# Adjacency blocks stored with the identity on their diagonal, and 16-bit operands for the put-off counts, in a four-layer graph network

## The chip, the cores and the metric

The kernel runs on one core of a Trainium2 chip. The metric is the device time of one execution in microseconds (us). The times shown are of nine executions, and one further execution was profiled.

A core has five engines that run side by side, each with its own queue of instructions that it takes in order. TensorE (PE in the profile) multiplies matrices; a matmul has a weight load (PEld) ahead of it, which can overlap the matmul before. VectorE (DVE), ScalarE (ACT) and GpSimd (POOL) work on tiles of 128 partitions. SyncE (SP) issues transfers; ScalarE and GpSimd issue some too. The transfers themselves run on 16 DMA engines. Results of matmuls land in PSUM, which has eight banks per partition; everything else on the chip lies in SBUF.

## The reference

The input is `x` (4096 rows of 256 features) and a symmetric 0/1 matrix `adj` (4096 x 4096) whose diagonal is all ones. Four layers follow one another, each with a residual sum and a LayerNorm:

```python
x = _layernorm(x + _L0_gnn_ref(x, adj, L0_gnn_W, L0_gnn_b))
x = _layernorm(x + _L1_gnn_ref(x, adj, W1, W2, W3, U1, U2, ln_g, ln_b))
x = _layernorm(x + _L2_gnn_ref(x, adj, adj, L2_gnn_weight, L2_gnn_bias))
x = _layernorm(x + _L3_gnn_ref(x, adj, L3_gnn_W, L3_gnn_b))
```

- Layer 0: `agg = adj @ x / deg`, then `relu([x, agg] @ W + b)`.
- Layer 1, two steps: `Xf = R @ Xf` with `R` the rows of `adj + I` divided by their sums, and `Xa = A @ Xa`, where `A` is the softmax of bilinear attention logits cut to the smallest set of entries that holds 0.9 of each row, and renormalised. `Z` sums `Xf @ U1[n].T + Xa @ U2[n].T`; the layer ends with its own LayerNorm of `X + Z`.
- Layer 2: `[x, adj @ x, e] @ weight + bias`, where `e_i = sum_j adj_ij adj_ji`.
- Layer 3: `A_hat = adj + I`, normalised on both sides by the square root of its row sums, times `x`, then `relu(. @ W + b)`.

So layers 1 and 3 need `adj + I`, layers 0 and 2 need `adj` alone.

## The kernel before

There are 32 row tiles of 128 rows (`NT`), and `adj` is taken in blocks of 128 x 128. A product with `adj` is always made in the same way. The right-hand side is split in two halves of fewer bits each, laid side by side as 512 columns of the type `fp32r`. The 0/1 blocks, transposed, are the weights. So one row tile is 32 matmuls of 128x512, one for each block of its row of `adj`, which add up in one PSUM bank; the two halves of 256 columns are then added.

**The order of the work.** The program text is written tile by tile, but the order of each engine's queue is set when the program is built, from dependencies, the order in the text and reckoned durations. A queue's order can therefore differ from the text's, and the profile shows the order that came out. Waits between engines, and for buffers to be free again, are added by the builder.

**Layer 0** (`l0_main`, L271, and the loop at L338). For each tile `it`, GpSimd issues two transfers (L276) that read the tile's blocks from HBM as 32-bit numbers and write them to SBUF as 8-bit ones, `a8`; one transfer brings blocks 0 to 15, the other blocks 16 to 31. Nine buffers serve the `a8` tiles and, at the start, the tiles of `x`. SyncE stores each half to `adj8_d` in HBM (L277), from where the later layers read it. ScalarE casts 8 blocks at a time to `fp32r` (L281), PE multiplies (L173), and DVE counts the ones of each column (`column_counts`, L287) on the 8-bit tile. `l0_degrees` (L304) turns the counts into degrees by a small 16-bit matmul (L306). `l0_agg` (L317, DVE) reads the PSUM bank of the finished product; two banks (`acc`, `nef`) take turns. `l0_end` (L323) makes the LayerNorm: `ln_stats` (L188) computes mean and variance on DVE and takes the variance to the power -0.5 on GpSimd (`rstd`, L197); `ln_apply` (L200) on DVE waits for it. SyncE then stores `x1` and `x1b` (L331, L332). `l0_keys` makes attention keys of a tile two turns later.

**Layer 1** (`run_step`, L941, twice). `pieces` (L720) interleaves, in eight groups, the attention logits of the tile after next, the attention product of the current tile, and the product with `adj + I` of one tile (`neighbours`, L674). `neighbours` reads `adj8_d` (L678), casts it on ScalarE (L680) and multiplies (L683); after the last group it adds one more matmul, with the identity `ident_r` as weights (L685), which turns `adj` into `adj + I`. In step 0 it also makes `adj @ adj` for the diagonal block (L693), of which `r_end` (L700) takes the diagonal (L707) as `nef`, the `e_i` of layer 2. In step 0 the attention product uses the 16 largest entries of each row, whose rows GpSimd gathers from HBM (`gather`, L666, eight slots `G`); in step 1 it is a dense product (L766). 

`pick` (L531) marks rows for which this did not suffice in `bad`, a 0/1 column. `flag` (L579) counts them: two matmuls with one column each, with the weights `ones_sq` (how many in the tile, L589) and `before` (how many ahead of each row, L590), all 32-bit. The profile shows each of them as two records. The rows are put on a list (L603) and done later, 128 at a time (`put_off`, L894). PE takes part in `flag` in the midst of its other work, so it waits for `bad` when that is late.

At the end of step 1, beside the put-off rows of the list, `zu_tile` (L874) makes for every tile the products of its layer 2 input with two parts of the weight: SyncE loads the tile, PE transposes and multiplies (`zu`, L862, into 512 columns), ScalarE copies the result from PSUM to one of four slots `out` (L871), and SyncE stores it to `zu_d` (L878). For put-off rows the store is a GpSimd scatter (L787). Columns 0 to 255 are what `adj` multiplies in layer 2; columns 256 to 511 are the tile's own part `u`.

**Layers 2 and 3** (from L1101). `load_halves` reads the first half of `zu_d` and splits it. `main` (L1121) multiplies with the blocks of `adj8_d` (`piece`, L1102). `l2_end` (L1126) adds `u` and the `nef` term and makes the LayerNorm. `l2_y` makes the right-hand side of layer 3, `y`. `l3_end` (L1154) scales the product, and adds the tile's own `y` in two steps (the two halves, L1160 to L1162), since layer 3 needs `adj + I`; the loop at L1161 has three DVE steps of which the third adds the second half of the product.

## Time and profile before

| what | us |
|---|---|
| median of nine executions (3236.24 to 3254.3) | 3243.18 |
| the profiled execution's own time | 3243.96 |
| its span, first to last instruction | 3242.3 |
| PE busy | 2956.1 |
| DVE busy | 2289.4 |
| ACT busy | 1745.5 |
| POOL busy | 786.7 |
| mean granted TensorE clock | 0.966 of full speed |

By stages, from the trace: layer 0 is over after some 350 us, step 0 of layer 1 runs to about 1300, the change from step 0 to step 1 to about 1440, step 1 with its put-off rows to 2700, layer 2 to 2997 and layer 3 to the end.

How to read it: busy times are of one execution, and a busy PE is not PE at its peak, since matmuls are pipelined and the records of neighbours overlap. In a timeline row the first number is the start in us from the span's start and the second the duration of the row, which may be several instructions ("x4"); what stands in brackets is how long the engine was idle before it and what ended that. The name in "L276" is the kernel's line. Transfers that an engine issues are shown at their issue, not at their landing. A share over the whole span mixes stages with different limits, so each part of a change is read in its own stage.

### The profile page before, as it was taken

Reading aid. Unit: us, or ns where it says so; the run is one execution under the profiler, and the core shown is the slowest. Engines: PE = TensorE matmul, PEld = TensorE weight load, DVE = VectorE, ACT = ScalarE, POOL = GpSimd, SP = SyncE. Lnnn points to the kernel's source line nnn. Section 1 sums busy time; section 2 is a strip of 40 time slices with the busy share of each in tenths; the row PEclk is TensorE's granted clock in tenths of the full one; section 3 lists DMA queues with packets and bytes.
Section 4 is the critical chain, followed back from the end, with each engine's and each line's share of the span. In section 5 each row is a group of like instructions: output and inputs, shape, how many; then the busy total and the mean of one; then the engine's idle time right before and its main releaser. Section 6 shows DMA issues by size and latency. Waiting matters only on the chain. (4 is left out here: it accounts for less than half of the span.)

```text
span 3242.3 us, 45754 instructions
## 1 busy us (share of the span) xinstructions
PE 2956.1 (91%) x14376; PEld 2333.2 (72%) x14376; DVE 2289.4 (71%) x7161; ACT 1745.5 (54%) x2906; POOL 786.7 (24%) x915
## 2 busy tenths in 40 slices
PE   7999889999999996799989899999999796999998
PEld 3788667777777774577877777877788554887886
DVE  4566778888888785268979896989799663444444
ACT  3555655566656563375545454645555334666664
POOL 1121256676666664000000001000100100000000
PEclk9999999999999997899999999999999898999999
DMA  9995467778777774320001110011011234333332
GB/s 169 157 176 118 85 108 141 141 147 141 140 139 140 138 137 130 110 67 22 24 25 27 30 38 27 29 35 38 25 35 29 64 125 132 108 109 102 104 110 81
DMA packets 247872, 300.14 MB, mean 93 GB/s; under 512 B 34688, under 2 KB 201536, under 8 KB 247616
## 3 DMA queue, kind: packets, MB, share of 16 engines
q0 software_dynamic: 46576, 104.94, 23.1%
q1 hardware_dynamic: 188800, 180.93, 18.7%
q10 hardware_dynamic: 12240, 11.23, 1.1%
q8 instruction: 116, 1.90, 0.3%
q14 instruction: 140, 1.15, 0.2%
HBM read 331.17 MB, written 66.45 MB: 123 GB/s over the span
## 5 line engine op out<-in xcount | busy, mean ns | idle before, releaser
L683 PE MATMUL acc_r<-xh,adjq 128*128 128x512 f32 x2048 | 609.6, 428 | 30.0 <-ACT adjq L680 16.0
L766 PE MATMUL acc_bank<-xa,at 128*128 128x256 f32 x2304 | 568.6, 387 | 28.8 <-ACT at L744 28.3
L669 POOL DMA_INDIRECT G<-x_d,cols x512 | 496.8, 970 | 279.4 <-PE acc_bank L758 148.2
L680 ACT CAST adjq<-adj 128x512 fp32r<-128x512 fp8e4 x512 | 316.4, 620 | 392.3 <-PE acc_r L683 304.8
L766 PEld LDWEIGHTS acc_bank<-xa,at 128*128 128x128 f32 x2304 | 424.0, 194 | 90.1 <-ACT at L744 39.1
L683 PEld LDWEIGHTS acc_r<-xh,adjq 128*128 128x128 f32 x2048 | 376.3, 191 | 126.2 <-ACT adjq L680 46.0
L197 POOL TENSOR_TENSOR rstd<-ve,mhalf 128x1 f32<-128x1 f32 x168 | 103.1, 614 | 1345.1 <-DVE ve L195 1237.4
L430 DVE MAX8 cand<-e 128x8 f32<-128x256 f32 x1024 | 382.5, 413 | 65.0 <-ACT e L412 63.7
L412 ACT COPY e<-lg 128x512 f32<-128x512 f32 x552 | 319.6, 585 | 198.4 <-PE lg L411 194.7
L411 PE MATMUL lg<-kS,q 128*128 128x512 f32 x1104 | 399.8, 447 | 4.8 <-ACT e L412 4.8
L758 PE MATMUL acc_bank<-G,dg 128*128 128x256 f32 x1024 | 288.0, 398 | 76.8 <-DMA G<-x_d,cols 61.3
L1106 ACT CAST a<-a 128x1024 fp32r<-128x1024 fp8e4 x256 | 268.0, 1048 | 157.7 <-PE acc L173 121.5
L758 PEld LDWEIGHTS acc_bank<-G,dg 128*128 128x128 f32 x1024 | 194.1, 195 | 133.0 <-DMA G<-x_d,cols 77.9
L527 DVE FIND_INDEX8 cols<-top,e 128x8 uint32<-128x4096 f32 x64 | 282.8, 4418 | 0.0
L173 PE MATMUL acc<-xh,a 128*128 128x512 f32 x1024 | 255.6, 403 | 21.6 <-DMA a<-adj_d 16.1
L173 PE MATMUL acc<-y0h,a 128*128 128x512 f32 x1024 | 253.6, 400 | 0.0
L173 PEld LDWEIGHTS acc<-xh,a 128*128 128x128 f32 x1024 | 191.7, 190 | 64.0 <-ACT xh L149 23.7
L173 PE MATMUL acc<-yh,a 128*128 128x512 f32 x1024 | 233.7, 390 | 0.0
L744 ACT COPY at<-at_ps 128x512 f32<-128x512 f32 x296 | 173.5, 588 | 99.8 <-PE at_ps L741 98.3
L185 ACT COPY xt<-tr 128x256 f32<-128x256 f32 (+1 forms) x268 | 111.9, 425 | 204.6 <-PE tr L183 187.8
L173 PEld LDWEIGHTS acc<-yh,a 128*128 128x128 f32 x1024 | 192.1, 188 | 39.7
L173 PEld LDWEIGHTS acc<-y0h,a 128*128 128x128 f32 x1024 | 187.9, 188 | 42.1 <-issue 0.6
(287 smaller groups left out, 4587.4 us busy)
## 6 DMA issues: line engine op xcount, KB each, us to landing
adj<-adj_d SPq DMA_DIRECT2D x256, 128.0 KB
a<-adj_d SPq DMA_DIRECT2D x256, 128.0 KB
a<-in_adjt POOLq DMA_DIRECT2D x64, 256.0 KB
adj_d<-a SPq DMA_DIRECT2D x64, 256.0 KB
adjn<-in_adjn POOLq DMA_DIRECT2D x64, 256.0 KB
x_d<-x SPq DMA_DIRECT2D x64, 128.0 KB
xf_d<-xf_new SPq DMA_DIRECT2D x64, 128.0 KB
G<-x_d,cols POOLq DMA_INDIRECT x512
```

The costliest lines, as they stand in the source:

```text
L173: nc.tensor.matmul(acc, a[:, j, :], halves(jt), start=(jt == 0), stop=(jt == NT - 1))
L411: nc.tensor.matmul(pl[:, :LC], q[k], kS[:, s], start=(k == 0), stop=(k == 1))
L412: nc.scalar.copy(l[:, s], pl[:, :LC])
L430: nc.vector.max(dst[:, 8 * g : 8 * g + 8], src[:, g * GW : (g + 1) * GW])
L527: nc.vector.max_index(st["at"][:, 8 * r : 8 * r + 8], t8, st["e"][:, :N])
L669: nc.gpsimd.indirect_dma_start(out=g, out_offset=None, in_=x1_d, in_offset=bass.IndirectOffsetOnAxis(ap=st["at"][:, k : k + 1], axis=0))
L680: nc.scalar.copy(a, cur["a8"][:, g % 2 * GP : (g % 2 + 1) * GP, :])
L683: nc.tensor.matmul(acc_r, a[:, j, :], xf[:, jt, :], start=(jt == 0), stop=False)
L744: nc.scalar.copy(at[:, :G, :], ps[:, :G, :])
L758: nc.tensor.matmul(acc_a, dg[:, k % 4, :], st["G"][k], start=(k == 0), stop=(k == KEPT - 1))
L766: nc.tensor.matmul(acc_a, ats[g][:, j, :], cur["xa"][:, jt, :], start=(jt == 0), stop=(jt == NT - 1))
L1106: nc.scalar.copy(a, a8)
```

## The change

The diagonal block of each row of `adj` is stored to `adj8_d` with the identity added, so that what the later layers read is `adj + I`. GpSimd adds it in 8-bit numbers (`loop`, from `a8` and `ident8`), and SyncE writes the block over the one just stored. Layer 0 itself keeps using `a8`, which is `adj` alone. What follows from it:

- The attention steps drop the identity matmul, and with it `ident_r`; the last of the 32 block matmuls now ends the sum.
- Layer 3 drops the two DVE steps that added the tile's own `y`.
- Layer 2 and `nef`, which need `adj` alone, have the surplus taken out: `zu` subtracts, on GpSimd, the columns 0 to 255 from the columns 256 to 511 before they are stored, so that `u` carries the correction; and a DVE step in layer 0 takes the diagonal of each tile (`own`), which is subtracted from `nef` ahead of layer 2.

Apart from this, `flag` copies `bad` to a 16-bit column on DVE, and `ones_sq` and `before` are 16-bit, so that its two matmuls have 16-bit operands.

```diff
--- before.py
+++ after.py
@@ -104,6 +104,7 @@
     dinv = const.tile([P, NT], F32, name="dinv")
     nef = const.tile([P, NT], F32, name="nef")
 
+    own = const.tile([P, NT], F32, name="own")
     wq_sb = const.tile([P, 2, 2 * DA], F32, name="wq_sb")
     w3t_sb = const.tile([P, 2, 2 * DA], F32, name="w3t_sb")
 
@@ -246,6 +247,8 @@
         x1 = xpool.tile([P, NT, D], F32, tag="X", name="x1")
         y0h = hpool.tile([P, NT, 2 * D], F32R, tag="H", name="y0h")
         deg1 = l0.tile([P, NT], F32, name="deg1")
+        ident8 = l0.tile([P, P], F8, name="ident8")
+        nc.gpsimd.tensor_copy(ident8, ident, saturate=False)
         ones_bf = l0.tile([P, 1], BF16, name="ones_bf")
         nc.vector.memset(ones_bf, 1.0)
 
@@ -275,6 +278,12 @@
             for s in (slice(0, NT // 2), slice(NT // 2, NT)):
                 nc.gpsimd.dma_start(a8[:, s, :], adjt[it, :, s, :])
                 nc.sync.dma_start(adj8_d[it][:, s, :], a8[:, s, :])
+            loop = l0w.tile([P, P], F8, tag="loop", name="loop")
+            nc.gpsimd.tensor_add(loop, a8[:, it, :], ident8, saturate=False)
+            nc.sync.dma_start(adj8_d[it][:, it, :], loop)
+            junk = l0w.tile([P, P], F32, tag="junk", name="junk", bufs=1)
+            nc.vector.scalar_tensor_tensor(junk, a8[:, it, :], 1.0, ident, op0=ALU.mult, op1=ALU.mult,
+                                           accum_out=own[:, it : it + 1])
 
             def piece(it, c):
                 a = l0w.tile([P, JP, P], F32R, tag="adjt", name="a", bufs=4)
@@ -356,14 +365,12 @@
 
         FIRST = [[range(k * NT // 16, (k + 1) * NT // 16) for k in range(2)]]
         FIRST.append([range(5 * NT // 32, 8 * NT // 32), range(8 * NT // 32, 11 * NT // 32)])
-        ones_sq = l1.tile([P, P], F32, name="ones_sq")
+        ones_sq = l1.tile([P, P], BF16, name="ones_sq")
         nc.vector.memset(ones_sq, 1.0)
 
-        before = l1.tile([P, P], F32, name="before")
+        before = l1.tile([P, P], BF16, name="before")
         nc.gpsimd.affine_select(before, ones_sq, pattern=[[1, P]], compare_op=ALU.is_gt, fill=0.0, base=0,
                                 channel_multiplier=-1)
-        ident_r = l1.tile([P, P], F32R, name="ident_r")
-        nc.vector.tensor_copy(ident_r, ident)
         upto = l1.tile([P, PAD], F32, name="upto")
         nc.gpsimd.iota(upto, pattern=[[1, PAD]], base=0, channel_multiplier=0, allow_small_or_imprecise_dtypes=True)
 
@@ -586,8 +593,10 @@
                 st["nb"] = small("nbad", 1, I32)[:1, :]
                 nc.scalar.copy(st["nb"], pb[:1, :1])
                 return
-            nc.tensor.matmul(pb[:, 0:1], ones_sq, st["bad"], start=True, stop=True)
-            nc.tensor.matmul(pb[:, 1:2], before, st["bad"], start=True, stop=True)
+            bad = small("bad16", 1, BF16)
+            nc.vector.tensor_copy(bad, st["bad"])
+            nc.tensor.matmul(pb[:, 0:1], ones_sq, bad, start=True, stop=True)
+            nc.tensor.matmul(pb[:, 1:2], before, bad, start=True, stop=True)
             sofar, slot = small("sofar"), small("slot")
             nc.vector.tensor_add(sofar, later["base"], pb[:, 0:1])
 
@@ -680,9 +689,7 @@
             nc.scalar.copy(a, cur["a8"][:, g % 2 * GP : (g % 2 + 1) * GP, :])
             for j in range(GP):
                 jt = g * GP + j
-                nc.tensor.matmul(acc_r, a[:, j, :], xf[:, jt, :], start=(jt == 0), stop=False)
-            if g + 1 == NLC:
-                nc.tensor.matmul(acc_r, ident_r, xf[:, i, :], start=False, stop=True)
+                nc.tensor.matmul(acc_r, a[:, j, :], xf[:, jt, :], start=(jt == 0), stop=(jt == NT - 1))
             if pn is not None:
                 if g % (NLC // 2) == 0:
                     cur["b8"] = cur["w"].tile([P, NT // 2, P], F8, tag="adjn8", name="adjn8", bufs=2)
@@ -869,6 +876,7 @@
             out = z["out"][:, z["n"] % 4, :]
             z["n"] += 1
             nc.scalar.copy(out, ps)
+            nc.gpsimd.tensor_sub(out[:, D:], out[:, D:], out[:, :D])
             return out
 
         def zu_tile(i):
@@ -1108,6 +1116,7 @@
 
         ahead = [piece(0, c) for c in range(NJP)]
         zh = load_halves(l23.tile([P, 4 * J0 * D], F32, name="scratch"), zu_d[:N, :], nc.sync, slice(0, D))
+        nc.vector.tensor_sub(nef, nef, own)
         w2e_sb = load_bcast(l23, w2[2 * D, :], "w2e_sb")
         b2_sb = load_bcast(l23, b2, "b2_sb")
         w3_sb = load_w(l23, w3, "w3_sb")
@@ -1157,9 +1166,7 @@
             a = l23.tile([P, D], F32, tag="agg", name="agg", bufs=2)
             d = dinv[:, it : it + 1]
             nc.scalar.activation(a, acc[:, :D], AF.Copy, scale=d)
-            own = y_halves(it).bitcast(F32)
-            for part in (own[:, :D], own[:, D:], acc[:, D:]):
-                nc.vector.scalar_tensor_tensor(a, part, d, a, op0=ALU.mult, op1=ALU.add)
+            nc.vector.scalar_tensor_tensor(a, acc[:, D:], d, a, op0=ALU.mult, op1=ALU.add)
             nc.vector.tensor_add(a, a, b3_sb)
             nc.vector.scalar_tensor_tensor(a, a, 0.0, x3, op0=ALU.max, op1=ALU.add)
             o = l23.tile([P, D], F32, tag="h", name="o", bufs=3)
```

## The prediction

> **What bounds the kernel now.** I read the page first for its sums, then busy time by stage, then the chain of waits for what ends last, then the queues of SyncE and GpSimd in layer 0, then single instructions of the edited lines.
>
> ```profile
> span 3242.3 us, 45754 instructions
> PE 2956.1 (91%) x14376; PEld 2333.2 (72%) x14376; DVE 2289.4 (71%) x7161; ACT 1745.5 (54%) x2906; POOL 786.7 (24%) x915
> ...
> 119.00:335.00 216.00, 216.00 (x1023) 174.19 (x1022) 139.25 (x578) 121.40 (x157) 35.36 (x64) 1.00 0.83 147
> 400.00:1130.00 730.00, 673.84 (x3722) 532.61 (x3721) 588.23 (x1765) 432.45 (x834) 481.23 (x510) 0.98 0.76 138
> 1440.00:2540.00 1100.00, 1012.63 (x5103) 837.39 (x5102) 946.27 (x3134) 565.98 (x946) 87.26 (x106) 0.97 0.12 29
> 2569.00:2658.00 89.00, 82.61 (x290) 45.41 (x289) 69.92 (x152) 35.28 (x75) 8.14 (x5) 1.00 0.40 138
> ```
>
> Each stretch shows the busy time of PE, PEld, DVE, ACT, POOL, then clock, DMA share and GB/s. Layer 0's main loop (119 to 335 us) has no PE gap at all. The attention steps (400 to 1130, 1440 to 2540) have PE at 92%, with waits. The stretch in which the ZU tiles are made (2569 to 2658) has PE at 93% and DVE at 79%. The chain names what ends last near the end of step 1 and of the kernel:
>
> ```profile
> 2698.14 3.20 DMA zu_d<-e,to_l
> ...
> 2998.56 230.09 PE acc L173 x1015
> ...
> 3229.18 0.49 DVE agg L1162
> 3229.70 0.50 DVE agg L1162
> ```
>
> So layer 3 is 1015 matmuls back to back, 0.227 us each, and only the last tile's DVE work follows them. The wait that I think decides lies in layer 0:
>
> ```profile
> 98.19 1.07 POOL L276 DMA_DIRECT2D a<-in_adjt  x2 [10.91 <-ACT a L281]
> 145.80 1.11 POOL L276 DMA_DIRECT2D a<-in_adjt  x2 [4.19 <-ACT xt L185]
> 149.32 0.56 POOL L197 TENSOR_TENSOR rstd<-ve,mhalf 128x1 f32<-128x1 f32 x1 [2.41 <-DVE sums L299]
> 154.06 1.10 POOL L276 DMA_DIRECT2D a<-in_adjt  x2 [4.17 <-ACT xt L185]
> ...
> 106.42 0.32 SPq L277 DMA_DIRECT2D adj_d<-a  x1
> 152.74 4.46 SPq L277 DMA_DIRECT2D adj_d<-a  x2
> 157.29 0.45 SPq L331 DMA_DIRECT2D x_d<-x  x1
> ...
> 237.66 0.47 DVE L320 SCALAR_TENSOR_TENSOR agg<-acc,rdeg,agg 128x256 f32<-128x256 f32 x1
> 243.47 0.17 PE L306 MATMUL acc_bank<-ones_bf,counts 128*128 128x1 bf16 x1
> ```
>
> Counting the pairs at L276, the one at 98.19 loads tile 10 and the one at 145.80 tile 16; the next follows 8.26 us later, one tile of PE work. L277 stores each half as it lands, so SyncE shows the landings: tile 10's second half at 106.42 (8.2 us after its issue), tile 16's halves at 152.74 and, since an issue takes 0.32 us, at 157.20 - 0.32 = 156.88 (6.9 and 11.1 us). The load of tile 17 is issued at 154.06, before tile 16 has all landed. GpSimd waits for no landing here: its queue holds only loads and the `rstd` powers.
>
> **Layer 0: the added wait.** The new `tensor_add` on GpSimd reads block `it` of the tile just loaded: the first half for tiles 0 to 15, the second for 16 to 31. Where does it stand in the queue? The order on each queue is set when the program is built, by reckoned times. The store at 157.29 is x1 of tile 6 (the seventh since 104.00), and it stands behind both stores of tile 16, ten tiles ahead of it; so the builder reckons tile 16 landed before LayerNorm 6 ends, thus before the load of tile 17. The add needs the same landing as that store, so I place it ahead of the next load in GpSimd's queue. Behind it then wait the next load and the next `rstd` power (L197), behind that power DVE's `ln_apply` (L202) and all that follows it in DVE's order, among it the next tile's `l0_agg` (L319, L320), and for that PE waits, since a tile's PSUM bank serves the tile after next.
>
> For tiles below 16 the add is free at 6.9 us, inside the 8.26. From 16 on a turn is landing plus add. With one load in flight the landing lies between tile 10's 8.2 us (lighter traffic) and tile 16's 11.1; I take 9.4. The add is not in the trace; the nearest two-input row on GpSimd is the power of one column, 0.55 us, and I allow 0.9 with its semaphores (0.3, a one-input `affine_select` of 128x128, to 1.5). A turn is 10.3 us against 8.26: 2.04 more, over the 15 turns from 16 to 31, 31 us. DVE may lag: L320 ends at 238.13 and the bank is wanted at 243.5, so 5 us are free, 6 with the last turn's. That leaves +25 us. Ends: with a turn of 9.1 us 13 - 6 = +7; with 12.0 us 56 - 6 = +50; if the add lands behind the next load, 0. Here stalled PE time is lost, as the loop has no gap to give back; the loads' nine-tile lead does not help, because it is the power, not the data, that comes late.
>
> The rest of layer 0 I put at nothing: the multiply with `accum_out` on DVE is the L707 row (0.27 + 0.08 us), 32 times 11 us on a DVE that is 64% busy in a loop PE bounds; without that cover 11 us. It too waits for the landing, but only shifts DVE within the 5 us. The 32 block stores are one more SyncE issue (0.32 us) each, with x1 and x1b behind them, which nobody reads before step 0.
>
> **Attention: what goes.**
>
> ```profile
> L685 PE MATMUL acc_r<-xh,ident_r x64: 388/389/582, 386.5 to 2499.2; 128*128 128x512 f32 x64
> ...
> 827.17 0.34 PE L589 MATMUL mm_bank<-bad,ones_sq 128*128 128x1 f32 x2
> 827.37 0.36 PE L590 MATMUL mm_bank<-bad,before 128*128 128x1 f32 x2
> 827.59 0.70 PE L411 MATMUL lg<-kS,q 128*128 128x512 f32 x2
> ...
> 839.65 0.70 PE L758 MATMUL acc_bank<-G,dg 128*128 128x256 f32 x2 [0.84 <-DMA G<-x_d,cols]
> ```
>
> The identity product lasts 0.389 us, but matmuls overlap: a 128x512 one in a stream costs 0.227 us, so 64 of them give 14.5 us, not 25. A put-off count is four records of PE work, 0.42 us from 827.17 to 827.59, 0.105 each. With 16-bit operands I count two; the 16-bit count matmul of L306 lets its successor start 0.03 us later (152.68 to 152.71). Two at 0.03 to 0.105 save 0.21 to 0.36 us; at 0.27, 64 give 17 us. Against it: the `bad` copy on DVE (a one-column copy, L544, takes 0.14 us), which comes between `bad` and the matmul. In step 1 PE waits for `bad` some 20 times, about 1 us each; 0.2 us more on each is 4 us. Ceiling: -14.5 - 17 + 4 = -27.5 us.
>
> Not all arrives. In step 0 PE waits 28 times for gathered rows, 35.9 us in all, and those gathers stand in a GpSimd queue with 0.3 us between them; the wait at 839 comes just after the identity product at 835.6, so its 7 us there go into that wait. Of the flags' 8.6 us I let half through: -4. In step 1 DVE is 86% busy and several waits are DVE's: 70% of 7.3 + 8.6, less the 4, is -7. Together -11 (ends -27.5 and +4, all saved time absorbed and the copies paid).
>
> **ZU and layers 2, 3.** `zu` gains a 128x256 subtraction on GpSimd between ScalarE's copy and the store. 32 of them lie in 89 us beside PE; four output slots cover some 9 us of delay. Cover gone, the store's slot and then the PSUM bank wait for it. A GpSimd operation can be held up by DVE:
>
> ```profile
> 2589.49 4.51 DVE L495 SCALAR_TENSOR_TENSOR spare_row<-e,pr_l 128x4096 uint8<-128x4096 f32 x1
> 2589.81 4.61 POOL L197 TENSOR_TENSOR rstd<-ve,mhalf 128x1 f32<-128x1 f32 x1
> ```
>
> The same power takes 0.55 us elsewhere. Ends 0 and +16 (below); +3 taken. One subtraction is on the chain, before the indirect store at 2698.14: +0.8. In layer 3 two of three DVE steps go: in the last tile 0.49 + 0.50 with gaps, -1.0; the other 31 lie beside PE. `nef - own` is one small DVE step while DVE awaits its first ZU rows: 0.
>
> [...]
>
> **Sum.** +25 - 11 + 3 + 0.8 - 1.0 = +17 us on the profiled execution (3243.96 us, 1.66 around its span of 3242.3; the median of nine is 3243.18, 0.8 less). So 3243.2 + 17 = 3260 us.
>
> **Rivals.** *No stall in layer 0* (faster): the add stands behind the next load, or the landing with one load in flight is so short that PE's 5 us cover it. For it: loads land at 8.2 us when traffic is light, and the lead in data is 60 us. Against: SyncE's order. The rest is -11 + 3 - 0.2 = -8, 3235 us; a better hit on the attention waits gives 3220.
> *The saving does not arrive* (the change does not do what it says): PE's 0.5 us per tile go into the waits for gathers and for `bad`, and layer 0 holds: 3243 + 3 = 3246, within 0.2%. For it: the 28 gather waits; against it: 92% PE.
> *DVE locks GpSimd out in the ZU stretch* (slower): place L871, when a subtraction starts under one of the eight 4.4 us DVE steps there (five probes, three match-and-replace). Each long step then passes one subtraction instead of two at the 2.3 us pace: eight too few, 18 us, and with it the stores, output slots and PE; less what slots cover, +16; from about five held subtractions on it decides. With layer 0 unharmed -11 + 16 = +5, up to 3256. Against it: in 168 powers only one took 4.6 us. [...]
>
> **Chances.** Forecast 0.50 (own range 3245 to 3290), no stall 0.35, no saving 0.10, lock-out 0.05. The range 3228 to 3288 leaves out the best of the second and the worst of the first. Under 0.2% (6.5 us) nine runs cannot tell a change from none. Faster: 0.31 of the second, 0.04 of others, 0.35; slower: 0.44 of the first, 0.06 of others, 0.50; the rest, 0.15, is within.
>
> **What would show it.** Layer 0: GpSimd idle before the add, released by the load of `a`; L276 pairs over 9 us apart from tile 17 on; PE gaps after tile 8 or so, and the first attention work some 25 us later. Attention: no L685, L589 and L590 with half the records and 95 ns weight loads (L306's), PE's waits for `G` longer. ZU: GpSimd steps of 0.6 us or, if held, 4 us. The forecast is wrong if the L276 pairs stay 8.3 us apart with the add in between, or if the loop keeps its 8.26 us though they do not.

## The result: 0.5% faster beside the kernel before, and 0.7% slower on another chip

The changed kernel took 3231.01 us (median of ten executions, 3223.63 to 3239.68). The kernel before, run beside it on the same chip, took 3247.94 us (31 executions). The ratio is 0.9951, with a 95% interval of 0.9937 to 0.9964: 17 us faster, where 17 us slower was forecast. Run again on another chip (e6_after below), the same kernel was slower, 3309.72 against 3282.9 us, ratio 1.0071 [1.0044, 1.0099]. Each set of runs was made on one chip, and chips differ: in the six sets of this document the kernel before took 3218, 3247, 3248, 3282, 3283 and 3293 us. So a kernel is compared only with the kernel before of its own set, as a ratio.

The page of the changed kernel, and its busy time in the four stretches shown of before:

```profile
span 3235.7 us, 45409 instructions
PE 2936.6 (91%) x14184; PEld 2296.4 (71%) x14184; DVE 2276.1 (70%) x7225; ACT 1737.3 (54%) x2906; POOL 830.3 (26%) x982
...
119.00:335.00 216.00, 190.27 (x842) 148.31 (x841) 120.61 (x523) 96.83 (x129) 44.08 (x83) 0.97 0.87 145
400.00:1130.00 730.00, 682.58 (x3772) 532.69 (x3772) 621.32 (x1854) 455.71 (x886) 484.65 (x522) 0.97 0.80 142
1440.00:2540.00 1100.00, 1002.66 (x5064) 827.47 (x5063) 948.29 (x3170) 568.49 (x947) 90.88 (x109) 0.97 0.13 30
2569.00:2658.00 89.00, 74.03 (x262) 42.04 (x261) 62.98 (x121) 27.41 (x62) 35.02 (x34) 0.96 0.36 123
```

In layer 0 (first row) PE is now busy for 190 of 216 us; before, it was busy for all 216. GpSimd has 67 instructions more (982 against 915). The stretches are fixed in time while the stages have moved, so the other rows do not hold quite the same work as before.

Where the time went is read from the first and last records of each stage; each row runs from the record that ends the row above. The first pair of columns is from the two profiles first shown (whose chips may differ); the second is from two profiles on one chip, e5_before and e6_after.

| stage, from which record to which | before | changed | | before, one chip | changed, same chip | |
|---|---|---|---|---|---|---|
| layer 0: start to last degree matmul | 350.8 | 398.0 | +47.2 | 350.6 | 399.7 | +49.1 |
| step 0: to last `G` product | 927.8 | 877.7 | -50.1 | 966.0 | 950.8 | -15.2 |
| change of step: to first dense product | 150.0 | 137.3 | -12.7 | 151.9 | 135.0 | -16.9 |
| step 1: to last issue of `list_d` | 1105.2 | 1100.7 | -4.5 | 1107.3 | 1101.6 | -5.7 |
| to last `zu` matmul | 162.7 | 167.9 | +5.2 | 162.3 | 167.0 | +4.7 |
| to layer 2's first matmul | 16.9 | 17.4 | +0.5 | 19.0 | 18.5 | -0.5 |
| layer 2: to layer 3's first matmul | 279.1 | 284.1 | +5.0 | 278.1 | 282.7 | +4.6 |
| layer 3: to its last matmul | 235.7 | 239.7 | +4.0 | 235.7 | 239.8 | +4.1 |
| to the end | 14.1 | 12.9 | -1.2 | 14.0 | 12.9 | -1.1 |
| span | 3242.3 | 3235.7 | -6.6 | 3284.9 | 3308.0 | +23.1 |

Layer 0 lost nearly twice what was forecast, and step 0 gained far more. Whether the sum is above or below nothing hangs on step 0, which gained 50 us in one pair and 15 in the other.

**Layer 0.** GpSimd's timeline in the changed kernel, and then DVE's in the same stretch:

```profile
177.83 0.52 POOL L282 TENSOR_TENSOR loop<-a,ident 128x128 fp8e4<-128x128 fp8e4 x1 [3.96 <-DMA a<-in_adjt]
178.30 1.11 POOL L279 DMA_DIRECT2D a<-in_adjt  x2
183.44 0.56 POOL L198 TENSOR_TENSOR rstd<-ve,mhalf 128x1 f32<-128x1 f32 x1 [4.03 <-DVE ve L196]
187.73 0.46 POOL L282 TENSOR_TENSOR loop<-a,ident 128x128 fp8e4<-128x128 fp8e4 x1 [3.73 <-DMA x0i<-in_x]
188.22 1.12 POOL L279 DMA_DIRECT2D a<-in_adjt  x2
193.28 0.57 POOL L198 TENSOR_TENSOR rstd<-ve,mhalf 128x1 f32<-128x1 f32 x1 [3.94 <-DVE ve L196]
```

```profile
193.10 0.19 DVE L308 TENSOR_TENSOR sums<-sums 128x64 uint16<-128x64 uint16 x1
197.31 0.29 DVE L285 SCALAR_TENSOR_TENSOR junk<-a,ident 128x128 f32<-128x128 fp8e4 x1 [4.02 <-DMA a<-in_adjt]
...
197.53 0.50 DVE L203 TENSOR_SCALAR x<-agg,bn,rstd 128x256 f32<-128x256 f32 x1
```

The add (L282) stands ahead of the next pair of loads (L279) and waits 4 us for a landing. From 168.19 to 313.47 us the pairs come 145.28 / 14 = 10.4 us apart; 10.3 was forecast. But DVE waits too: its `own` step (L285) stands ahead of `ln_apply` (L203) and is held some 4 us by the same landing, although the power that `ln_apply` needs was done at 193.85 us. That power, in turn, waits here for DVE (`ve`) and not behind the add. The waits between 100 and 400 us (total, times, longest) show both; "issue" is a wait for nothing that the profile shows, here in front of the same add:

```profile
DVE junk L285 <- DMA a<-in_adjt: 95.0, 23, 5.8
POOL loop L282 <- issue: 71.1, 16, 6.4
POOL loop L282 <- DMA a<-in_adjt: 34.3, 6, 6.6
```

**The counts.** A put-off count in step 0 of the changed kernel:

```profile
706.16 0.47 PE L418 MATMUL lg<-kS,q 128*128 128x512 f32 x1
706.48 0.18 PE L598 MATMUL mm_bank<-bad,ones_sq 128*128 128x1 bf16 x1
706.52 0.16 PE L599 MATMUL mm_bank<-bad,before 128*128 128x1 bf16 x1
706.54 0.48 PE L418 MATMUL lg<-kS,q 128*128 128x512 f32 x1
```

Two records where there were four; the next matmul starts 0.06 us after the first of them (0.42 us before).

**ZU.** GpSimd's subtraction, all 34 of them, and who waited for it; then a stretch of its timeline:

```profile
L879 POOL TENSOR_TENSOR e<-e x34: 712/726/4908, 2551.7 to 2683.4; 128x256 f32<-128x256 f32 x34
...
  ACT e L878: 16.6, 9
```

```profile
2569.49 6.33 POOL L879 TENSOR_TENSOR e<-e 128x256 f32<-128x256 f32 x3
2576.82 0.73 POOL L879 TENSOR_TENSOR e<-e 128x256 f32<-128x256 f32 x1 [1.00 <-ACT e L878]
2578.53 4.13 POOL L879 TENSOR_TENSOR e<-e 128x256 f32<-128x256 f32 x1 [0.99 <-ACT e L878]
```

The DVE step (L502) under which the subtraction at 2578.53 was held, and another kind of long DVE step (L664) with a subtraction that ran under it:

```profile
2577.60 4.49 DVE L502 SCALAR_TENSOR_TENSOR spare_row<-e,pr_l 128x4096 uint8<-128x4096 f32 x1
...
2615.97 4.43 DVE L664 MATCH_REPLACE8 e<-match_l,e 128x4120 f32<-128x4120 f32 x1
...
2618.50 0.73 POOL L879 TENSOR_TENSOR e<-e 128x256 f32<-128x256 f32 x1 [2.26 <-ACT e L878]
```

A subtraction takes 0.73 us (median; four took 1.1 to 1.6), but three of the 34 took 4.1 to 4.9, each while a DVE step of 4.5 to 5.4 us (L502, one of the five probes that the prediction counts) ran; each of the three ended just under 0.6 us after that step. Under the three match-and-replace steps of 4.4 us (L664), which begin between 2611 and 2621 us, six subtractions took their usual 0.72 to 0.73. ScalarE waited for a slot nine times, 16.6 us in all. From the first to the last `zu` matmul it is 135.3 us where it was 126.7; how much of this the three held ones make was not separated.

### The profile page after: what moved, and what is told of

It reads as the page before. It is cut to its first block, busy times and chain, and to the rows that moved or that the text cites. A ratio compares the mean times of both kernels' runs of the same rounds, so it can differ in the third digit from the quotient of the medians.

```text
span 3235.7 us, 45409 instructions
## 1 busy us (share of the span) xinstructions
PE 2936.6 (91%) x14184; PEld 2296.4 (71%) x14184; DVE 2276.1 (70%) x7225; ACT 1737.3 (54%) x2906; POOL 830.3 (26%) x982
## 5 line engine op out<-in xcount | busy, mean ns | idle before, releaser
L692 PE MATMUL acc_r<-xh,adjq 128*128 128x512 f32 x2048 | 621.4, 433 | 32.8 <-ACT adjq L689 23.4
L1114 ACT CAST a<-a 128x1024 fp32r<-128x1024 fp8e4 x256 | 267.9, 1048 | 167.0 <-PE acc L174 127.6
L765 PE MATMUL acc_bank<-G,dg 128*128 128x256 f32 x1024 | 280.9, 393 | 48.8 <-DMA G<-x_d,cols 42.9
L418 PEld LDWEIGHTS lg<-kS,q 128*128 128x128 f32 x1104 | 185.2, 192 | 24.9 <-ACT e L419 11.6
```

Of the source, the lines that this page charges most:

```text
L418: nc.tensor.matmul(pl[:, :LC], q[k], kS[:, s], start=(k == 0), stop=(k == 1))
L692: nc.tensor.matmul(acc_r, a[:, j, :], xf[:, jt, :], start=(jt == 0), stop=(jt == NT - 1))
L765: nc.tensor.matmul(acc_a, dg[:, k % 4, :], st["G"][k], start=(k == 0), stop=(k == KEPT - 1))
L1114: nc.scalar.copy(a, a8)
```

## The experiments

Theory S, from the prediction: GpSimd's add makes layer 0's loss. Rival D: DVE's `own` step makes it. For step 0: theory F, the 16-bit counts; I, the identity matmul; O, the order that the builder makes of the queues; P, PE's time alone. Ratios are to the kernel before on the same chip.

| run | median us | kernel before | ratio [95%] |
|---|---|---|---|
| e1_flag16 | 3196.47 | 3218.45 | 0.9935 [0.9920, 0.9950] |
| e2_flag32 | 3224.32 | 3218.45 | 1.0023 [1.0012, 1.0034] |
| e3_add_dve | 3196.64 | 3218.45 | 0.9937 [0.9922, 0.9952] |
| e4_no_ident | 3167.13 | 3218.45 | 0.9845 [0.9830, 0.9860] |
| e5_before | 3285.22 | 3282.9 | 1.0000 [0.9980, 1.0019] |
| e6_after | 3309.72 | 3282.9 | 1.0071 [1.0044, 1.0099] |
| e7_own_late | 3286.19 | 3282.9 | 1.0002 [0.9986, 1.0018] |
| e8_both_late | 3263.89 | 3282.9 | 0.9941 [0.9918, 0.9964] |
| e10_before | 3247.86 | 3246.6 | 1.0000 [0.9982, 1.0017] |
| e11_no_ident | 3189.07 | 3246.6 | 0.9825 [0.9807, 0.9843] |
| e9_best | 3175.63 | 3246.6 | 0.9787 [0.9768, 0.9807] |
| e12_pad64 | 3258.04 | 3246.6 | 1.0043 [1.0027, 1.0059] |
| e14_before | 3283.67 | 3282.16 | 1.0001 [0.9975, 1.0027] |
| e13_ident_first | 3267.36 | 3282.16 | 0.9953 [0.9930, 0.9977] |
| e16_first_flag16 | 3255.19 | 3282.16 | 0.9907 [0.9882, 0.9932] |
| e15_best | 3253.1 | 3282.16 | 0.9911 [0.9888, 0.9934] |
| e17_ident_first | 3266.76 | 3293.26 | 0.9921 [0.9900, 0.9941] |
| e18_no_ident | 3255.77 | 3293.26 | 0.9885 [0.9862, 0.9908] |

### e1_flag16 and e2_flag32: the counts alone, and the change without them

e1 is the kernel before with only this part of the change; e2 is the changed kernel with the "-" lines in place of the "+" lines.

```diff
-        ones_sq = l1.tile([P, P], F32, name="ones_sq")
+        ones_sq = l1.tile([P, P], BF16, name="ones_sq")
...
-        before = l1.tile([P, P], F32, name="before")
+        before = l1.tile([P, P], BF16, name="before")
...
-            nc.tensor.matmul(pb[:, 0:1], ones_sq, st["bad"], start=True, stop=True)
-            nc.tensor.matmul(pb[:, 1:2], before, st["bad"], start=True, stop=True)
+            bad = small("bad16", 1, BF16)
+            nc.vector.tensor_copy(bad, st["bad"])
+            nc.tensor.matmul(pb[:, 0:1], ones_sq, bad, start=True, stop=True)
+            nc.tensor.matmul(pb[:, 1:2], before, bad, start=True, stop=True)
```

> The kernel before with one part of the change: `flag` copies `bad` to a 16-bit column, and `ones_sq` and `before` are 16-bit. Step 0 became 51 us shorter in the changed kernel (first to last matmul with `G`: 865.7 to 814.7 us), where the prediction had let 4 us through. Theory F (the 16-bit counts make that gain): 40 to 55 us under the kernel before, about 3200 us. Theory I (the identity matmul's removal makes it): 0 to 10 us under it, about 3243. Theory O (neither by itself; the builder's new order of the queues does it): anything within 25 us of the kernel before, with a step 0 whose order of matmuls differs from both.

> The changed kernel with the 32-bit counts of before (`ones_sq`, `before`, `bad` as before, no copy). Theory F: the gain of step 0 goes and the stall in layer 0 stays, 40 to 50 us above the changed kernel, about 3275 us. Theory I: 0 to 10 us above it, about 3237. Theory O: anything between.

The 16-bit counts are worth 22 us by themselves, less than theory F's 40 to 55 and more than theory I's 0 to 10. These 22 us are what is left after layers 2 and 3 became longer, by some 7 us according to e12 below. The rest of the change, without the counts, is 6 us slower than the kernel before. So theory F is not the 51 us: step 0 of e2, which has 32-bit counts, was 798.7 us from first to last product with `G`. The counts show in step 1 (first dense product to last issue of `list_d`: 1089.6 us in e1, 1106.7 in e2). The changed kernel was not run on this chip; at 0.9951 of the kernel before it would take an estimated 3203 us, 22 less than e2.

### e4_no_ident and e11_no_ident: the identity product alone

```diff
-                nc.tensor.matmul(acc_r, a[:, j, :], xf[:, jt, :], start=(jt == 0), stop=False)
-            if g + 1 == NLC:
-                nc.tensor.matmul(acc_r, ident_r, xf[:, i, :], start=False, stop=True)
+                nc.tensor.matmul(acc_r, a[:, j, :], xf[:, jt, :], start=(jt == 0), stop=(jt == NT - 1))
```

> The kernel before without the identity matmul of the attention steps: R is adj alone there, so the identity's term is left out. Theory I: 40 to 55 us under the kernel before, about 3200. Theory F: 0 to 10 us under it; the prediction's term is 7 us of PE work in each step, of which 4 us in all were to arrive from step 1. Theory O: within 25 us of the kernel before, with another order of step 0's matmuls.

> The kernel before without the identity matmul of the attention steps (R is adj alone there, the identity's term is left out), now beside a profile of the kernel before on the same chip. Theory I: 35 to 55 us under the kernel before, most of it between the first and the last matmul with `G`, although PE is spared only 32 x 0.23 = 7 us there. Rival P (only PE's time arrives): 7 to 15 us under it.

It is 51 us under the kernel before on one chip and 58 on the other, where the product costs an estimated 64 x 0.227 = 14.5 us of PE (0.227 us is what one of layer 3's 1015 matmuls takes). On the second chip a profile of the kernel before was taken beside it:

> The kernel before, unchanged, for a profile on the same chip as the runs beside it. No theory sees a difference to the kernel before. The kernel before has taken 3218, 3248 and 3283 us on three chips, and its step 0 (first to last matmul with `G`) 865.7 and 900.2 us in two profiles, with layer 0 and step 1 within 3 us: so step 0 should be what differs here too.

From its first to its last product with `G` the kernel before takes 872.6 us, the one without the identity product 813.1. Theory I holds against F, and rival P's 7 to 15 us do not cover it. Of these 59 us, 31 are waits of PE for `G`: over all of step 0 they fall from 67.7 us (46 times) to 36.9 (20 times). The product's own time is an estimated 7 (32 x 0.227), and the rest was not separated. Between 560 and 1120 us PE's busy time rises from 519.3 to 551.0 of the 560 us, at a granted clock of 1.00 where it was 0.99. Not every stage gained: in the rows of the first table step 0 is 58.0 us shorter than in e10_before and the change of step 9.5, but step 1 is 11.7 us longer (1115.7 against 1104.0), with 32 products fewer.

Where the waits for `G` come from is seen in PE's queue. First the kernel before (e10_before), from the last piece of a tile on:

```profile
784.62 1.28 PE L683 MATMUL acc_r<-xh,adjq 128*128 128x512 f32 x4
785.74 0.39 PE L685 MATMUL acc_r<-xh,ident_r 128*128 128x512 f32 x1
...
786.71 1.02 PE L758 MATMUL acc_bank<-G,dg 128*128 128x256 f32 x4
787.58 0.39 PE L693 MATMUL nef_ps<-adjn,adj 128*128 128x128 fp8e4 x4
787.77 0.70 PE L411 MATMUL lg<-kS,q 128*128 128x512 f32 x2
788.31 0.59 PE L758 MATMUL acc_bank<-G,dg 128*128 128x256 f32 x2
790.33 0.70 PE L758 MATMUL acc_bank<-G,dg 128*128 128x256 f32 x2 [1.43 <-DMA G<-x_d,cols]
...
793.73 2.20 PE L683 MATMUL acc_r<-xh,adjq 128*128 128x512 f32 x8
```

Now the same place without the product (e11_no_ident):

```profile
769.62 1.28 PE L683 MATMUL acc_r<-xh,adjq 128*128 128x512 f32 x4
...
771.50 1.02 PE L756 MATMUL acc_bank<-G,dg 128*128 128x256 f32 x4
772.18 1.28 PE L683 MATMUL acc_r<-xh,adjq 128*128 128x512 f32 x4
773.30 0.40 PE L691 MATMUL nef_ps<-adjn,adj 128*128 128x128 fp8e4 x4
773.50 0.71 PE L411 MATMUL lg<-kS,q 128*128 128x512 f32 x2
774.05 1.21 PE L756 MATMUL acc_bank<-G,dg 128*128 128x256 f32 x4
774.91 1.28 PE L683 MATMUL acc_r<-xh,adjq 128*128 128x512 f32 x4
```

Behind the identity product the builder put two groups of `G` with no block matmuls (`acc_r`) between them, and the eight that belong there in one place at 793.73. GpSimd issues one gather every 0.95 + 0.30 us (the instruction and the gap before the next), so two slots of `G` (one group of four matmuls) every 2.5 us. In e10_before PE wants groups at 783.94, 786.71 and 788.31: the third 1.6 us after the second. PE waits for the gather. In e11_no_ident four block matmuls stand behind each group, the two groups shown are 2.55 us apart, and PE does not wait. Between 560 and 1120 us PE's waits for `G` fall from 40.6 us (31 times) to 8.9 (8 times).

### e13_ident_first and e17_ident_first: the same work, another order

```diff
+            if g == 0:
+                nc.tensor.matmul(acc_r, ident_r, xf[:, i, :], start=True, stop=False)
             for j in range(GP):
                 jt = g * GP + j
-                nc.tensor.matmul(acc_r, a[:, j, :], xf[:, jt, :], start=(jt == 0), stop=False)
-            if g + 1 == NLC:
-                nc.tensor.matmul(acc_r, ident_r, xf[:, i, :], start=False, stop=True)
+                nc.tensor.matmul(acc_r, a[:, j, :], xf[:, jt, :], start=False, stop=(jt == NT - 1))
```

> The kernel before with the identity matmul moved from the end of a tile's 32 block matmuls to their start; the same matmuls, the same PE work, the same result. In the order that the builder makes of it, four block matmuls stand behind every group of two `G` products, as in the kernel without the identity matmul; in the kernel before, two groups of `G` follow each other without them and eight stand in one place. Theory O (that order makes the gain of step 0: `G` is then taken no faster than GpSimd brings it): 35 to 55 us under the kernel before, that is the 57 us of the kernel without the product less some 7 to 15 for the product itself. Rival P (PE's time or the product itself makes it): within 10 us of the kernel before.

> The kernel before with the identity matmul first, once more, now beside the kernel without that matmul on the same chip. On a chip whose kernel before takes about 3283 us (step 0 some 900 us) it gave 15 us where 35 to 55 were expected. Theory O with the rest of the gain taken by the chip: on a chip at about 3218 to 3248 us 35 to 55 us under the kernel before; on one at about 3283 us 10 to 20 again. In both cases the kernel without the matmul is only the product's own time below it, 7 to 20 us. Rival P: within 20 us of the kernel before on any chip, and 35 us or more above the kernel without the matmul on a fast one.

> The kernel before without the identity matmul (R is adj alone there, the identity's term is left out), beside the kernel that has it first. Theory O: 7 to 20 us under the kernel with the matmul first, whatever the chip. Rival P: 35 us or more under it on a fast chip.

These runs fell on chips where the kernel before takes 3282 and 3293 us. On the first the gain was 15 us, less than theory O's 35 to 55 and more than rival P's 10: not settled by that run. On the second the same kernel gave 26 us, more than either theory had said for such a chip (O 10 to 20, P up to 20), and the kernel without the product, beside it, gave 38. The two lie 11 us apart, in theory O's 7 to 20. So on that chip 26 of 38 us come with all the PE work still in place: order, not PE's time. On a chip where the kernel before is at 3218 or 3247 us this order was not run. Against e14_before, in the profiles, e13_ident_first has step 0 shorter by 29.1 us and the change of step by 10.4, and step 1 longer by 16.6: the new order helps the gathers and costs time in step 1.

In e13_ident_first four block matmuls stand behind each group of `G`:

```profile
795.32 1.02 PE L758 MATMUL acc_bank<-G,dg 128*128 128x256 f32 x4
796.00 1.28 PE L685 MATMUL acc_r<-xh,adjq 128*128 128x512 f32 x4
...
798.32 1.03 PE L758 MATMUL acc_bank<-G,dg 128*128 128x256 f32 x4
799.00 1.28 PE L685 MATMUL acc_r<-xh,adjq 128*128 128x512 f32 x4
```

Beside it a profile of the kernel before was taken:

> The kernel before, unchanged, for a profile on the same chip as the runs beside it: step 0 between 865 and 900 us as in its three profiles so far, PE waiting some 30 times for `G` between 560 and 1120 us.

Its step 0 (904.9 us) was just above that, and its PE waited for `G` 16 times, 16.2 us, half as often as expected. In e13_ident_first that wait is 2.0 us, but PE now waits elsewhere (560 to 1120 us):

```profile
PE acc_r L682 <- DVE m L463: 15.0, 17, 2.7
...
PE lg L411 <- issue: 11.1, 14, 0.9
...
PE acc_bank L758 <- DMA G<-x_d,cols: 2.0, 2, 1.0
```

The first two, 26 us, are not among PE's waits of e11_no_ident in that window, on the chip at 3247 us. The changed kernel has them on the chip at 3283 (e6_after: 10.9 us each), where step 0 gained 15 us and not 50: the waits for `G` have been replaced there by these. What makes them differ between chips was not tried, and stays open.

### e3_add_dve, e7_own_late, e8_both_late: layer 0

e3 has the add on DVE in the same place of the text. e7 and e8 let the steps wait for the tile's degree, since min(block, max(degree, 1)) is the block; e7 does it with `own` only, e8 with both, on DVE. The lines of the changed kernel in place of which these stand go from `l0_main`; they are not shown.

```diff
 e3_add_dve
-            nc.gpsimd.tensor_add(loop, a8[:, it, :], ident8, saturate=False)
+            nc.vector.tensor_add(loop, a8[:, it, :], ident8, saturate=False)
 e7_own_late, e8_both_late: in l0_degrees
+            dm = work.tile([P, 1], F32, tag="dm", name="dm")
+            nc.vector.tensor_scalar(dm, deg, 1.0, None, op0=ALU.max)
+            nc.vector.reciprocal(rd, dm)
...
+            junk = l0w.tile([P, P], F32, tag="junk", name="junk", bufs=1)
+            nc.vector.scalar_tensor_tensor(junk, a8[:, it, :], dm, ident, op0=ALU.min, op1=ALU.mult,
+                                           accum_out=own[:, it : it + 1])
 e8_both_late only
+            loop = l0w.tile([P, P], F8, tag="loop", name="loop")
+            nc.vector.scalar_tensor_tensor(loop, a8[:, it, :], dm, ident, op0=ALU.min, op1=ALU.add, saturate=False)
+            nc.sync.dma_start(adj8_d[it][:, it, :], loop)
```

> The changed kernel with the 8-bit add of layer 0 on DVE in place of GpSimd. Theory S (the add stands in GpSimd's queue between a load and the next, and with it come the 38 us that layer 0's loop lost): the L279 pairs come 8.3 us apart again, the last degree matmul is back from 398 to 355 to 365 us, and the kernel is 25 to 45 us under the changed one, about 3195 us. Rival (DVE then waits for the same landing, and its counts, `l0_agg` and LayerNorm stand behind it): layer 0 stays over 385 us and the time within 10 us of the changed kernel.

e3's last degree matmul was at 385.2 us, 13 below the changed kernel's (398.0, in another set of runs), not back at 355 to 365. DVE now waits, in front of the add, for landings (30.0 us) and for the store of an earlier block (53.3 us, 14 times). So the add's place on GpSimd cannot be all of it; the rival has its point.

> The kernel before, unchanged, for a profile on the same chip as the runs beside it. No theory sees a difference to the kernel before; what is wanted is its step 0 (865.7 us from first to last matmul with `G` in the profile shown). Theory I (the identity matmul's removal shortens step 0): about 840 us here, 40 to 50 us over the changed kernel of this call. Rival C (much of the 51 us was the chip, not the kernel): within 20 us of it.

> The changed kernel, unchanged, on the same chip as the kernel before. By the first comparison 0.995 of the kernel before. Step 0 by theory I some 795 us, with the last degree matmul of layer 0 near 398 us.

These two give the right-hand columns of the first table. e6's step 0 took 887.5 us from first to last product with `G` and e5's 900.2, 13 apart and far from the 795 of theory I: rival C was right on this chip, and the expected ratio of 0.995 was not met.

> The changed kernel with the DVE step that makes `own` put off: it takes the smaller of the block and the degree (at least one), which changes no value but makes it wait for the degree, and so stand behind the tile's counts and not right behind the load. GpSimd's add stays. Theory S (GpSimd's add, ahead of the next load and the `rstd` powers, is what costs layer 0 its 47 us): within 10 us of the changed kernel, the last degree matmul still after 390 us. Rival D (DVE's 95 us of waiting in front of the `own` step, 23 times for a load to land, is what costs): 25 to 45 us under the changed kernel, the last degree matmul before 365 us.

> The changed kernel with both steps, `own` and the add, on DVE behind the tile's degree, so that no engine waits for a landing and the block's store comes long after the store under it. Theories S and D both: layer 0 is back to 350 to 360 us, GpSimd's queue as before, and the kernel is 35 to 50 us under the changed one, 50 to 65 under the kernel before (about 3160 us where the kernel before takes 3218). If layer 0's loss comes from the third store of each tile (SyncE's queue), it stays over 380 us and the time within 15 us of the changed kernel.

The last degree matmul: 399.7 us with both steps at the landing (e6), 375.5 with `own` late (e7), 354.5 with both late (e8), 350.6 in the kernel before (e5). The times fall with it: 3309.72, 3286.19, 3263.89 us. So both S and D hold, about half each: `own` on DVE costs 24 us, the add on GpSimd 21, and 4 remain; e7 lies between the two windows, 24 us under the changed kernel. Of the 24 us, 10 are lost by the first tile's end: the first degree matmul comes at 105.5 us in e6 and 95.4 in e7. e8 is 46 us under the changed kernel, as expected, but only 19 under the kernel before, where 50 to 65 were: on this chip the changed kernel was not the faster of the two. The third store of each tile is still there in e8, so the store by itself is not what cost the time. In e7, where DVE no longer waits for the landing, the power behind the add is what it waits for (20.5 us in e5_before, also 32 times):

```profile
DVE x L203 <- POOL rstd L198: 90.5, 32, 5.7
```

GpSimd's order there, from tile 17 on, is add, load, power, as the prediction had it:

```profile
201.42 0.41 POOL L282 TENSOR_TENSOR loop<-a,ident 128x128 fp8e4<-128x128 fp8e4 x1 [7.42 <-issue]
202.01 1.11 POOL L279 DMA_DIRECT2D a<-in_adjt  x2 [0.17 <-issue]
203.14 0.57 POOL L198 TENSOR_TENSOR rstd<-ve,mhalf 128x1 f32<-128x1 f32 x1
```

The pairs of loads come 9.8 us apart from there on (172.36 to 309.05 us, 14 turns). The long turns begin earlier, with the one from 120.60 to 131.88 us, between the loads of tiles 12 and 13.

### e12_pad64: layers 2 and 3

```diff
+    pad = work.tile([P, 16], F32, tag="pad", name="pad", bufs=1)
+    nc.vector.memset(pad, 0.0)
```

> The kernel before with nothing but an unused tile of 64 bytes per partition in the pool `work`, which moves the tiles of layers 2 and 3 where the 16-bit `bad` column moved them. Every kernel with the 16-bit counts had layer 3 at 239.3 to 239.7 us from its first to its last matmul, every kernel without at 235.7, and layer 2 at 282 to 284 against 278. Theory A (the place of the tiles makes it): layer 3 239.7 us, layer 2 283. Rival B (the 16-bit matmuls themselves or the shorter program): 235.7 and 278.

An unused tile of 64 bytes makes the kernel before 0.43% [0.27, 0.59] slower. The last piece of the chain of waits is layer 3's stream of matmuls; first e10_before, then e12_pad64, on one chip:

```profile
3002.64 230.13 PE acc L173 x1015
```

```profile
3004.72 234.10 PE acc L175 x1015
```

The same 1015 matmuls take 0.2267 us each in the one and 0.2306 in the other, at a granted clock of 1.00 in both. Layer 2 went from 279.9 to 282.6 us (first matmul to layer 3's first). Theory A's numbers are met without a 16-bit matmul: the 64 bytes per partition are by themselves +4 us in layer 3 and +3 in layer 2. That they act by shifting other tiles, and that the `bad16` column shifts them as far, is the author's reading; no trace shows where a tile lies. The two make 7 of the 11 us that e12 is slower; where the others lie was not found.

### e9_best, e16_first_flag16 and e15_best: what to keep

e9_best (run again as e15_best) is e8 with one subtraction on the weight, where there were 34 on its products, and with the 64 bytes of e12. e16_first_flag16 is the kernel before with e13's order, the 16-bit counts and the 64 bytes.

```diff
+            nc.vector.tensor_sub(w[:, :, D:], w[:, :, D:], w[:, :, :D])
...
-            nc.gpsimd.tensor_sub(out[:, D:], out[:, D:], out[:, :D])
```

> The changed kernel with `own` and the add on DVE behind the degree, with the 34 subtractions of `zu` replaced by one subtraction of the two parts of the weight, and with 64 bytes more in the pool `work`. The subtractions cost 8 to 10 us (first to last `zu` matmul 126.7 to 135.2 us): that stretch is back to 127 us, and the kernel is 45 to 60 us under the changed kernel (which took 27 us more than the kernel before on one chip and 16 less on another), 25 to 60 us under the kernel before. If the subtractions were hidden, the stretch stays at 135 us.

> The kernel before with the identity matmul first, the 16-bit counts, and 64 bytes more in the pool `work`; nothing else of the change, so no add in layer 0 and no subtraction. If the parts add up (identity first 35 to 55, 16-bit counts 22 as measured): 55 to 75 us under the kernel before, as fast as the mended change beside it within 15 us. If theory O fails: 15 to 30 us under. Layer 3 is at 235.7 us if a shift by 128 bytes does not matter where one by 64 does, and at 239.7 if every shift does.

> The mended change once more (`own` and the add behind the degree, the subtraction done once on the weight, 64 bytes more), beside the kernel with the identity product first. It was 0.979 of the kernel before on one chip; on a chip where step 0 is slow it should keep less, 0.98 to 0.99.

e9_best is 71 us under the kernel before, where 25 to 60 were expected; the `zu` matmuls are back to 125.0 us from first to last, so the subtractions had cost some 9. On the chip at 3282 us (e15_best) it kept 29, a ratio of 0.991 where 0.98 to 0.99 was expected. e16_first_flag16, which has nothing of the diagonal blocks, took 27 us off there, not the 55 to 75 of theory O but what was named for its failing (15 to 30): within the intervals it equals e15_best. The parts of e16 add up as 15 (e13) and 12, less than the 22 of the counts in e1. e16, with `bad16` and the 64 bytes, by that reading a shift of 128, did not restore layer 3 (239.3 us), so it would not be the shift by 64 as such; which tile's place matters was not tried.

## Why the prediction was wrong

**The attention term is the step that failed.** It read: "the wait at 839 comes just after the identity product at 835.6, so its 7 us there go into that wait", and set the ceiling at PE's own time, -27.5 us. The wait did not follow the product by chance. The builder's order around the product makes it: in e10_before too, two groups of `G` follow the product with no block matmuls between them. Without the product that order is even, and most of the waits for `G` go as well. The identity product's removal was worth 51, 58 and 38 us on three chips, the counts 22 on one, where -11 was taken for both. The waits were also under-read: 28 times and 35.9 us are what a part of step 0 shows (500 to 1130 us), and all of it has 41 waits, 61.3 us. In step 1, where part of the -11 was to come from, the product's removal gave nothing: step 1 takes 1107.5, 1115.7 and 1118.1 us in the three kernels without it (e4, e11, e18), and 1103.1 to 1107.3 in four profiles of the kernel before.

**"The rest of layer 0 I put at nothing" failed too.** The multiply's 0.35 us were priced, and its wait named but said to move DVE only within 5 us. It cost 24 us (e6 to e7): in the changed kernel DVE stood still in it for 95 us between 100 and 400 us, ahead of `ln_apply`. Of the 24 us, 10 were lost by the first degree matmul (105.5 us in e6, 95.4 in e7). The argument used on GpSimd's queue in the same part (what stands behind a step that waits for a landing?) was not carried to DVE's.

**The add on GpSimd: the path was right, the exact size in part luck.** Its place ahead of the next load, and the power behind it that DVE waits for, are there in e7, where the add is left alone; layer 0 ends 24.9 us later than before, and +25 was forecast. But the turn there is 9.8 us and not 10.3, and the long turns begin at tile 12 and not 16: 19 turns from 120.60 to 309.05 us, 9.9 us each, against 8.26 before, are 31 us more, as were the forecast's 15 turns of 10.3. The 10.4 us of the changed kernel has DVE's wait in it as well. The add takes 0.41 to 0.54 us (median 0.46), where 0.9 was allowed, so the landing was later than reckoned.

**ZU was mis-sized:** +3 was taken, and the stretch grew by 8.6 us (126.7 to 135.3). What the lock-out rival described was there in three of 34 subtractions (4.1 to 4.9 us each), fewer than the five from which it was to decide, and under the probes alone: the match-and-replace steps, which the rival counted in, held none. What sets the probes apart from them no run here shows. Nor did any run show the price of a subtraction (0.8 us in the sum, 0.6 among the signs) when it was taken: the kernel before has none. Its measured median is 0.73 us.

**The small terms:** the end after layer 3 is 1.2 us shorter (1.0 forecast). The last subtraction, ahead of the indirect store, takes 0.71 us (0.8 forecast), but the changed kernel's chain of waits does not pass through it. Not in the sum at all: +7 us in layers 2 and 3 from 64 bytes (e12).

**The rivals.** "No stall in layer 0" gave 3235 us, close to the 3231 measured, for a reason that is false: the stall came at twice its size, so this is luck. "The saving does not arrive" is false on every chip. The direction came out wrong because attention gained 67 us in the first pair of profiles (the three rows from step 0 to step 1), six times the 11 taken, and that outweighed the errors that went the other way. On the chip at 3283 us it gained 38, and the kernel is 27 us slower; that this was the forecast direction is luck too, since every large term was off.

**Do the parts add up?** With the gains of the chip at 3218 us (-51 for the product, -22 for the counts), +49 for layer 0 and +9 for the subtractions they make -15, and -17 was measured. With those of the slow chips (-38 and -12) they make +8, where +27 was measured: what holds back step 0 there stays open.

## What to carry to other kernels

Where a builder sets the queues' order, price a removed instruction by the order that appears without it: look at what the engine does in the turn around it, above all at a bunched consumer that outruns its producer (here two groups 1.6 us apart, fed every 2.5 us). A step that reads a fresh load must be looked up in every engine's queue: whatever stands behind it waits for the landing (in the changed kernel 95.0 us of DVE's time and 34.3 of GpSimd's between 100 and 400 us). Tying both steps to a later value left 4 us of the 49 in layer 0 (e8). Before adding work for a saving, try the same work in another place: moving the identity product to the front of its sum gave 26 of the 38 us that removing it gave, with no other edit (15 us on another chip).

## What the runs showed of the hardware that was not expected

- Chips differ mostly in one stage. The kernel before took 865.7 to 904.9 us in step 0 in four profiles, while its layer 0 took 349.7 to 350.8, and layer 3 235.7 to 235.8. GpSimd's time for a gather does not tell them apart (median 0.946 to 0.949 us in all four), and the mean granted clock of the profiled execution hardly does (0.966 and 0.964 in the two faster profiles, 0.962 in both slower). A change's sign can depend on the chip: 0.9951 [0.9937, 0.9964] on one, 1.0071 [1.0044, 1.0099] on another.
- An unused tile of 64 bytes per partition changed the rate of a matmul stream: 0.2306 us per 128x512 product in layer 3 where it was 0.2267, 1.7% (e12).
